# Attention penalties in squares: two penalty products move from GpSimd to ScalarE

## The chip, the cores and the metric

The kernel runs on one core of one Trainium2 chip. The core has a matrix engine (PE), a vector engine (DVE), a scalar engine (ACT), GpSimd (POOL) and a queue that only issues transfers (SP); each works through its own instructions in order, and semaphores tie them together. The metric is the device time of one execution in microseconds, the median of several runs. Lower is better.

## The reference, cut to what matters

The network has four layers, each an attention-like part and a feed-forward part whose outputs are multiplied and added to the residual. The change touches the attention of the last layer only. In the kernel's shapes it handles 16 batches of 256 positions with 128 features in 16 heads of 8:

```python
g = jax.nn.sigmoid(hidden_states @ Wg + bg)
Z_I = g
Z_J = jnp.swapaxes(g, 1, 2)
res = (1.0 - Z_I) * jnp.maximum(1.0 - Z_I - Z_J, 0.0) + Z_I * jnp.minimum(1.0 - Z_I + Z_J, 1.0)
abs_ij = jnp.abs(idx[:, None] - idx[None, :])
scope = jnp.power(s - 2, 1.0 - g) + 2.0 - abs_ij
scope = jnp.clip(scope, 1e-32, 1.0)
log_pen = jnp.log(jnp.maximum(res * scope, 1e-32))
scores = jnp.einsum('bhqd,bhkd->bhqk', q, k) / np.sqrt(HEAD_DIM)
probs = jax.nn.softmax(scores + log_pen[:, None, :, :], axis=-1)
ctx = jnp.einsum('bhqk,bhkd->bhqd', probs, v)
```

One penalty matrix of 256 by 256 serves all 16 heads of a batch. The kernel never takes its logarithm: it multiplies the exponentials by the penalty.

## The kernel before, in words

`attn8` is the loop of all 8-feature attentions; the first layer uses it without a penalty, the last with one. It runs over heads: step `n` of 288 handles head `n` (16 heads a batch, 256 in all) and, 14 heads later, head `m = n - 14` in the second pass.

In step `n`, `scores` lets PE compute raw scores `pa` of head `n` (L345); DVE takes their negated row maxima `nmax` (L366). Once eight heads have their maxima, `shifted` turns them on PE (L387) and DVE adds them into the queries `qa` (L393). For head `m`, PE computes the shifted, transposed scores `pb` (L355) and ACT their exponentials `e` (L376). There are four `pa` and two `pb` buffers. `weaken` multiplies the exponentials of two heads, 128x1024 elements, by the penalty `pen` (L333): POOL does six of a batch's eight pairs, DVE the pairs that start at heads 2 and 8. `weigh` multiplies by the values on PE (L402), ACT copies the result `oT` (L413), and `turn` transposes and divides it (L428, L435, L436). `project` makes queries and keys for two batches: a matmul (L292), a copy on ACT (L299), a store `qkd` to DRAM (L301) and eight loads of `qT` or `kT` (L306), all transfers on the SP queue. `done` multiplies a finished batch by the gate on DVE (L1765) and adds it to the residual on POOL (L1766).

The penalty of batch `b + 1` is made while batch `b` runs. `penalty(b)` returns a list of steps, and the head loop takes one of them after a head's own work, in heads whose number `k` within the batch is in a fixed tuple:

```python
if k in (2, 3, 4, 5, 6, 7, 8, 9, 10, 11, 13, 14) and b + 1 < B:
    parts[b + 1].pop(0)()
elif k == 15 and b + 1 < B:
    pens[b + 1] = parts.pop(b + 1).pop(0)()
```

With `gi` the row of gates (a transfer replicates it over the partitions) and `gj` the negated gate of the partition's own position, the steps are: ACT forms `u = 1 - gi` (`rest`, L1693), `lo = relu(u + gj)` (`low`, L1696, two halves of 256), `hi = relu(gi + gj)` (`high`, L1699, two halves) and `hi = 1 - hi` (`rather`, L1702); POOL forms the distance term `sc` (`near`, L1705), `lo * u` and `hi * gi` (`inner`, L1708) and their sum (`summed`, L1711); DVE takes `pen = min(sc, 1) * lo` (`bounded`, L1715); ACT bounds it from below (`over`, `least_of`, L1719, L1722). A helper, `mixed`, rewrites an access so that the two halves of a row are read alternately, element 0, 256, 1, 257 and so on; `bounded` and the gate product of `done` use it.

A planner orders instructions outside the head loop by its own estimates, so the first two penalties, the setup of the stage and the first projection are interleaved with the last feed-forward work. Inside the loop `pin` fixes the order on every engine as the source writes it.

Of the kernel before, what the change touches and what calls it, by code (L numbers as in the profile page):

```python
# [10 lines left out]
F32 = mybir.dt.float32  # L11
I32 = mybir.dt.int32
BF16 = mybir.dt.bfloat16
AF = mybir.ActivationFunctionType
ALU = mybir.AluOpType
# [4 lines left out]
P = 128  # L20
B = 16
S = 256
D = 128
NT = B * S // P
# [60 lines left out]
def mixed(*tiles):  # L85

    axes = {2: "p (a b) -> p b a", 3: "p t (a b) -> p t b a"}
    return [t.rearrange(axes[len(t.shape)], a=2) for t in tiles]


class Net:
# [140 lines left out]
    def attn8(self, w, bias=None, wout=None, penalty=None, done=None):  # L232
# [12 lines left out]
        nc, tc = self.nc, self.tc  # L245
        scale = 1.0 / math.sqrt(8.0)
        LAG = 14
        H = 16 * B
        with ExitStack() as ctx:
            cp = ctx.enter_context(tc.tile_pool(name="at_c", bufs=1))  # L250
            pool = ctx.enter_context(tc.tile_pool(name="at", bufs=2))
# [18 lines left out]
            for j in range(4):  # L270
                q = cp.tile([P, 4, S], F32, name=f"qT{j}")
                nc.gpsimd.memset(q, 0.0)
                qbuf.append(q)
                k = cp.tile([P, 4, S], F32, name=f"kT{j}")
# [199 lines left out]
            for n in range(H + 4 * 8):  # L474
                i, u = divmod(n, 8)
                m = n - LAG
                if n < H or 0 <= m < H:
                    scores(n if n < H else None, m if 0 <= m < H else None)
                b, half = divmod(i, 2)
                if u == 1:  # L480
                    if is_step(i - 1):
                        shifted(i - 1)
                    if half == 1 and b + 1 < B:
                        values(b + 1)
                elif u == 3:
                    if is_step(i - 4) and penalty is not None:
                        turn(i - 4)
                    if is_step(i - 4) and (i - 4) % 2 == 1:
                        finish((i - 4) // 2)
                    if i % 4 == 2 and i // 4 + 1 < B // 2:  # L490
                        project(i // 4 + 1, 1)
                elif u == 5:
                    if is_step(i - 3):
                        weigh(i - 3)
                elif u == 7:
                    if is_step(i - 3) and penalty is None:
                        turn(i - 3)
                    if i % 4 == 1 and i // 4 + 1 < B // 2:
                        project(i // 4 + 1, 0)
                if done is not None and u in (4, 6) and is_step(i - 4) and (i - 4) % 2 == 1:  # L500
                    done((i - 4) // 2, u == 6)
                if penalty is not None:
                    k = n % 16
                    if k == 0 and b + 2 < B:
                        parts[b + 2] = penalty(b + 2)
                        parts[b + 2].pop(0)()
                    if k in (2, 3, 4, 5, 6, 7, 8, 9, 10, 11, 13, 14) and b + 1 < B:
                        parts[b + 1].pop(0)()
                    elif k == 15 and b + 1 < B:
                        pens[b + 1] = parts.pop(b + 1).pop(0)()  # L510
# [1146 lines left out]
    def attn3(self, g, dr, done):  # L1657


        nc, tc, a = self.nc, self.tc, self.a  # L1660
        with ExitStack() as ctx:
            cp = ctx.enter_context(tc.tile_pool(name="a3_c", bufs=1))
            pool = ctx.enter_context(tc.tile_pool(name="a3", bufs=1))
            pool2 = ctx.enter_context(tc.tile_pool(name="a3_2", bufs=2))
            pool3 = ctx.enter_context(tc.tile_pool(name="a3_3", bufs=3))
            dist = self.const("dist", cp, view="p (k q) -> p k q", k=2)
            least = cp.tile([P, 2], F32, name="least")
            nc.gpsimd.memset(least[:, 0:1], -1e-32)
            nc.gpsimd.memset(least[:, 1:2], 1e-32)
            wide = lambda t: t.rearrange("p (o q) -> p o q", o=1).to_broadcast([P, 2, S])  # L1670

            def penalty(b):

                rows = pool3.tile([P, 2, S], F32, name="rows")
                gi, pw = rows[:, 0, :], rows[:, 1, :]
                u = pool.tile([P, S], F32, name="u")
                lo = pool2.tile([P, 2, S], F32, name="lo")
                hi = pool2.tile([P, 2, S], F32, name="hi")
                sc = pool.tile([P, 2, S], F32, name="sc")
                pen = pool3.tile([P, 2, S], F32, name="pen")  # L1680
                gj = [g[:, 2 * b + k : 2 * b + k + 1] for k in range(2)]

                def fetch():
                    for j in range(2):
                        t = j * NT + 2 * b
                        nc.sync.dma_start(
                            rows[:, j, :],
                            dr[t : t + 2, :].rearrange("t p -> (t p)").partition_broadcast(P),
                        )


                def rest():
                    nc.scalar.activation(u, gi, AF.Identity, scale=-1.0, bias=1.0)  # L1693

                def low(k):
                    return lambda: nc.scalar.activation(lo[:, k, :], u, AF.Relu, bias=gj[k])  # L1696

                def high(k):
                    return lambda: nc.scalar.activation(hi[:, k, :], gi, AF.Relu, bias=gj[k])  # L1699

                def rather():
                    nc.scalar.activation(hi, hi, AF.Identity, scale=-1.0, bias=1.0)  # L1702

                def near():
                    nc.gpsimd.tensor_sub(sc, wide(pw), dist)  # L1705

                def inner(t, by):
                    return lambda: nc.gpsimd.tensor_mul(t, t, wide(by))  # L1708

                def summed():  # L1710
                    nc.gpsimd.tensor_add(lo, lo, hi)  # L1711

                def bounded():
                    to, near, inner = mixed(*(t.rearrange("p k q -> p (k q)") for t in (pen, sc, lo)))
                    nc.vector.scalar_tensor_tensor(to, near, 1.0, inner, ALU.min, ALU.mult)  # L1715


                def over():
                    nc.scalar.activation(pen, pen, AF.Relu, bias=least[:, 0:1])  # L1719

                def least_of():
                    nc.scalar.activation(pen, pen, AF.Identity, bias=least[:, 1:2])  # L1722
                    return pen

                return [
                    fetch, rest, low(0), low(1), high(0), high(1), rather, near,
                    inner(lo, u), inner(hi, gi), summed, bounded, over, least_of,
                ]

            self.attn8(  # L1730
                {n: a["L3_attn_W" + n] for n in "qkv"},
                bias={n: a["L3_attn_b" + n] for n in "qkv"},
                penalty=penalty,
                done=done,
            )


    def layer3(self, end, out):

        nc, tc = self.nc, self.tc
        X = self.xn
        right = lambda n, **kw: tc.tile_pool(name=n, bufs=1, side="right", **kw)
        with ExitStack() as ctx:
            gp = ctx.enter_context(right("a3_g"))
            dram = ctx.enter_context(tc.tile_pool(name="a3_d", bufs=1, space=DRAM))
            with right("f3_w") as cp:
                layers, load = self.local_weights(cp)
                with tc.tile_pool(name="l2_g", bufs=4) as got:  # L1750
                    gather = end["Ga"]
                    end["Ga"] = end["Gb"] = lambda: gather(got)
                    end["wb"] = end["wa"]
                    g, dr = self.local_layers(X, layers, load, end, lambda: self.gates3(gp, dram))
            for c in range(NT // 4):
                xc = X[:, 4 * c : 4 * c + 4, :]
                nc.scalar.activation(xc, xc, AF.Silu)

            def done(b, store):
                ts = slice(2 * b, 2 * b + 2)  # L1760
                if store:
                    nc.sync.dma_start(out[:, ts, :], self.x[:, ts, :])
                else:
                    attn, ffn = mixed(self.s[:, ts, :], X[:, ts, :])
                    nc.vector.tensor_mul(attn, attn, ffn)  # L1765
                    nc.gpsimd.tensor_add(self.x[:, ts, :], self.x[:, ts, :], self.s[:, ts, :])  # L1766

            self.attn3(g, dr, done)
# [516 lines left out]
```

## Time and profile before

| | us |
|---|---|
| median of 3 runs | 2729.04 |
| lowest and highest | 2728.78, 2735.28 |
| the profiled execution | 2734.26 |
| its span, first to last instruction | 2732.50 |
| PE busy | 2346.4 (86%) |
| DVE busy | 1962.1 (72%) |
| ACT busy | 1668.4 (61%) |
| POOL busy | 1384.6 (51%) |

The profile covers one execution. The durations below come from it, while times of kernels are compared by their medians; the profiled execution lies 5.2 us above the median. Busy shares are averages over layers with different limits, so the last attention is read by itself. A row of a group or a tile gives the engine, the line, the operation, the output and the inputs, and how long one instruction took. A row of waits names who waited, for whom, the total, how often, and the longest. In a timeline the two first numbers are start and duration, and brackets give the idle time before the instruction and who ended it. In a row of stretches the columns are the length, the busy time of PE, PE's weight loads, DVE, ACT and POOL with their counts, then the granted clock of PE as a share of full speed, the share of DMA and its rate.

### The profile page before, as it was taken

Reading aid. Unit: us, or ns where it says so; the run is one execution under the profiler, and the core shown is the slowest. Engines: PE = TensorE matmul, PEld = TensorE weight load, DVE = VectorE, ACT = ScalarE, POOL = GpSimd, SP = SyncE. Lnnn points to the kernel's source line nnn. Section 1 sums busy time; section 2 is a strip of 40 time slices with the busy share of each in tenths; the row PEclk is TensorE's granted clock in tenths of the full one; section 3 lists DMA queues with packets and bytes.
Section 4 is the critical chain, followed back from the end, with each engine's and each line's share of the span. In section 5 each row is a group of like instructions: output and inputs, shape, how many; then the busy total and the mean of one; then the engine's idle time right before and its main releaser. Section 6 shows DMA issues by size and latency. Waiting matters only on the chain.

```text
span 2732.5 us, 47736 instructions
## 1 busy us (share of the span) xinstructions
PE 2346.4 (86%) x17672; PEld 1560.2 (57%) x17735; DVE 1962.1 (72%) x3810; ACT 1668.4 (61%) x3680; POOL 1384.6 (51%) x1162
## 2 busy tenths in 40 slices
PE   6999997899756799999983789999999997889887
PEld 4666667566432455555561456666666665655554
DVE  6666633555579688888877899877776662788775
ACT  2555554233235466676641788888999896565653
POOL 3000001422417666666566667565654554798886
PEclk7999998899668899999996999999999998899987
DMA  3001002000114456556552000000000001121210
GB/s 84 24 29 33 17 17 101 6 11 12 35 54 152 142 165 196 180 182 189 173 185 57 21 22 23 15 19 18 24 11 11 13 14 32 33 46 30 49 30 9
DMA packets 136917, 168.25 MB, mean 62 GB/s; under 512 B 20850, under 2 KB 100604, under 8 KB 136684
## 3 DMA queue, kind: packets, MB, share of 16 engines
q1 hardware_dynamic: 128108, 147.09, 18.2%
q0 software_dynamic: 6496, 17.05, 1.8%
q8 instruction: 140, 2.29, 0.4%
q10 hardware_dynamic: 2080, 1.05, 0.1%
q14 instruction: 93, 0.76, 0.1%
HBM read 126.96 MB, written 29.79 MB: 57 GB/s over the span
## 4 chain that ended last, share of the span: by engine, by line
PE 27%; DVE 14%; ACT 11%; POOL 9%; issue 3%; DMA 2%; SPq 1%; POOLq 0%; DVEq 0%; ACTq 0%
PE py L1253 4%; ACT p L2033 3%; POOL e L333 3%; PE pm L2168 2%; PE pm L1922 2%; PE ps L2009 2%; PE ph L1496 2%; DVE pen L1715 2%; PE pa L1098 2%; PE pm L2096 1%; PE py L1519 1%; PE pb L355 1%; PE pa L345 1%; DVE sn L1948 1%; DVE ss L1944 1%
## 5 line engine op out<-in xcount | busy, mean ns | idle before, releaser
L366 DVE TENSOR_REDUCE nmax<-pa 128x2 f32<-128x512 f32 x512 | 329.6, 683 | 135.6 <-PE pb L355 109.1
L376 ACT ACTIVATE e<-pb 128x512 f32<-128x512 f32 x512 | 286.2, 594 | 226.8 <-PE pb L355 204.8
L355 PE MATMUL pb<-qa,kT 32*128 32x256 f32 x2048 | 388.4, 424 | 32.9 <-ACT e L376 32.9
L345 PE MATMUL pa<-kT,qT 32*128 32x256 f32 x2048 | 365.9, 435 | 10.9 <-DMA kT<-qkd 8.2
L1243 POOL TENSOR_TENSOR hc<-st,cn 128x1024 f32<-128x1024 f32 x111 | 261.2, 2353 | 193.7 <-DVE dbb L1226 120.9
L1230 DVE TENSOR_TENSOR_SCAN st<-dab,dbb 128x1024 f32<-128x1024 f32 x128 | 292.7, 2287 | 23.5 <-ACT dab L1216 8.1
L355 PEld LDWEIGHTS pb<-qa,kT 32*128 32x128 f32 x2048 | 249.8, 196 | 62.7 <-ACT e L376 54.0
L345 PEld LDWEIGHTS pa<-kT,qT 32*128 32x128 f32 x2048 | 231.4, 201 | 93.1 <-issue 56.2
L1253 PE MATMUL py<-hc,ident 128*128 128x512 f32 x512 | 270.6, 619 | 8.8 <-DVE hc L1243 7.4
L333 POOL TENSOR_TENSOR e<-e,pen 128x1024 f32<-128x1024 f32 x96 | 229.1, 2394 | 62.7 <-ACT e L376 61.5
L1922 PE MATMUL pm<-qkv,hT 128*128 128x512 f32 x384 | 211.9, 636 | 32.0 <-ACT p L2033 12.2
L2033 ACT ACTIVATE p<-ps,nm,rl 128x128 f32<-128x128 f32 x512 | 230.0, 474 | 12.2 <-DVE nm L2024 11.7
L1216 ACT ACTIVATE dab<-dl,A_log 128x512 f32<-128x512 f32 x256 | 177.7, 718 | 97.2 <-DVE st L1230 56.2
L178 POOL TENSOR_SCALAR ln_r<-ln_mv 128x4 f32<-128x4 f32 x32 | 8.5, 264 | 446.3 <-DVE ln_mv L189 438.6
L1957 POOL TENSOR_TENSOR rot<-rot,sn 128x512 f32<-128x512 f32 x128 | 162.6, 1274 | 125.7 <-DVE sn L1948 125.5
L1226 DVE TENSOR_TENSOR dbb<-du,bn 128x1024 f32<-128x1024 f32 x128 | 187.5, 1465 | 5.5 <-DMA bn<-dr 2.8
L2052 POOL TENSOR_TENSOR p<-p,den 128x512 f32<-128x512 f32 x128 | 130.5, 1041 | 39.7 <-DVE den L2047 30.7
L1253 PEld LDWEIGHTS py<-hc,ident 128*128 128x128 f32 x512 | 92.8, 197 | 80.7 <-issue 61.4
L1519 PEld LDWEIGHTS py<-w,h 128*128 128x128 f32 x752 | 101.1, 197 | 59.2 <-issue 39.7
L402 PE MATMUL pm<-e,vaug 128*32 128x256 f32 x2048 | 129.1, 394 | 3.6 <-DVE s L436 3.6
L1937 ACT ACTIVATE sq<-pm 128x512 f32<-128x512 f32 x128 | 76.4, 597 | 78.5 <-PE pm L1922 71.6
L1510 ACT ACTIVATE h<-ph,b1s 128x256 f32<-128x256 f32 x188 | 78.6, 470 | 70.0 <-PE ph L1496 69.1
(390 smaller groups left out, 5614.5 us busy)
## 6 DMA issues: line engine op xcount, KB each, us to landing
bn<-dr SPq DMA_DIRECT2D x64, 512.0 KB
cn<-dr SPq DMA_DIRECT2D x64, 512.0 KB
w<-in_L_ffn_W_dram SPq DMA_DIRECT2D x94, 256.0 KB
qkd<-qk SPq DMA_DIRECT2D x32, 256.0 KB
v<-v SPq DMA_DIRECT2D x64, 128.0 KB
f_y<-y SPq DMA_DIRECT2D x47, 128.0 KB
f_x<-zero POOLq DMA_DIRECT2D x8, 704.0 KB, 6.7
xr<-f_x SPq DMA_DIRECT2D x44, 128.0 KB
```

The costliest lines, as they stand in the source:

```text
L333: eng.tensor_mul(pairs[m], pairs[m], pen.to_broadcast([P, 2, 2, S]))
L345: nc.tensor.matmul(pa[:, t, :], qbuf[b % 4][r : r + 32, g, ts], kbuf[b % 4][r : r + 32, g, :], start=True, stop=True,)
L355: nc.tensor.matmul(pb[:, t, :], kbuf[b % 4][r : r + 32, g, ts], qas[m // 8][r : r + 32, g % 2, :], start=True, stop=True,)
L366: nc.vector.tensor_reduce(nbuf[n // 8 % 2][:, :, u // 4, u % 4, 8], pa, AX.X, ALU.max, negate=True)
L376: nc.scalar.activation(e, pb, AF.Exp, scale=scale)
L1216: nc.scalar.activation(d["da", r - r % 2][:, r % 2, :], d["dl"][:, h, :], AF.Exp, scale=an[:, h, n : n + 1])
L1226: mul = nc.vector.tensor_mul(db, du, d["bn", n])
L1230: nc.vector.tensor_tensor_scan(wide(d["st", r]), wide(d.pop(("da", r))), wide(db), 0.0, ALU.mult, ALU.add)
L1243: ins = eng.tensor_mul(d["hc", r], d.pop(("st", r)), d["cn", r // 4 * 2])
L1253: nc.tensor.matmul(d["py", h], self.ident, d["hc", r - r % 2][:, r % 2, :], start=(n == 0), stop=(n == N - 1))
L1922: nc.tensor.matmul(pj, hTs[b % 3][:, t * P : (t + 1) * P], rows[b]["l"]["qkv", j], start=True, stop=True,)
L2033: nc.scalar.activation(p[:, c, w, :], rows[b]["ps", u][i][:, c, w, :], AF.Exp, scale=rows[b]["r"][:, w, 0, h + 2 * c : h + 2 * c + 1], bia ...
```

## The change

With `h = gj / 2` and `gj` negative, `(1 - gi) * max(1 - gi + gj, 0)` equals `max((1 + h - gi)^2 - h^2, 0)`, and `gi * max(gi + gj, 0)` equals `max((gi + h)^2 - h^2, 0)`. So both inner terms become a Square with a bias per partition, followed by a Relu with a bias per partition, all on ACT; POOL takes their difference and adds `gi`. The three biases of each position are formed once in a small tile `sides`. The tile `u` and the steps `rest` and `rather` go away, and so do the two products on POOL. `over_none` is one step with two instructions. The list has one step less, so head 11 of a batch no longer takes one.

`bounded` and the gate product of `done` no longer use `mixed`: they read the same elements in plain order.

```diff
-                    if k in (2, 3, 4, 5, 6, 7, 8, 9, 10, 11, 13, 14) and b + 1 < B:
+                    if k in (2, 3, 4, 5, 6, 7, 8, 9, 10, 13, 14) and b + 1 < B:
...
+            sides = cp.tile([P, 3, NT], F32, name="sides")
+            nc.vector.tensor_scalar(sides[:, 0, :], g, 0.5, 1.0, ALU.mult, ALU.add)
+            nc.vector.tensor_scalar_mul(sides[:, 1, :], g, 0.5)
+            nc.vector.scalar_tensor_tensor(sides[:, 2, :], g, -0.25, g, ALU.mult, ALU.mult)
...
-                def rest():
-                    nc.scalar.activation(u, gi, AF.Identity, scale=-1.0, bias=1.0)
                 def low(k):
-                    return lambda: nc.scalar.activation(lo[:, k, :], u, AF.Relu, bias=gj[k])
+                    return lambda: nc.scalar.activation(
+                        lo[:, k, :], gi, AF.Square, scale=-1.0, bias=side(0, k)
+                    )
                 def high(k):
-                    return lambda: nc.scalar.activation(hi[:, k, :], gi, AF.Relu, bias=gj[k])
-                def rather():
-                    nc.scalar.activation(hi, hi, AF.Identity, scale=-1.0, bias=1.0)
+                    return lambda: nc.scalar.activation(hi[:, k, :], gi, AF.Square, bias=side(1, k))
+                def over_none(t):
+                    def f():
+                        for k in range(2):
+                            nc.scalar.activation(t[:, k, :], t[:, k, :], AF.Relu, bias=side(2, k))
+                    return f
...
-                def inner(t, by):
-                    return lambda: nc.gpsimd.tensor_mul(t, t, wide(by))
+                def less():
+                    nc.gpsimd.tensor_sub(lo, lo, hi)
                 def summed():
-                    nc.gpsimd.tensor_add(lo, lo, hi)
+                    nc.gpsimd.tensor_add(lo, lo, wide(gi))
                 def bounded():
-                    to, near, inner = mixed(*(t.rearrange("p k q -> p (k q)") for t in (pen, sc, lo)))
-                    nc.vector.scalar_tensor_tensor(to, near, 1.0, inner, ALU.min, ALU.mult)
+                    nc.vector.scalar_tensor_tensor(pen, sc, 1.0, lo, ALU.min, ALU.mult)
...
-                    fetch, rest, low(0), low(1), high(0), high(1), rather, near,
-                    inner(lo, u), inner(hi, gi), summed, bounded, over, least_of,
+                    fetch, low(0), low(1), over_none(lo), high(0), high(1), over_none(hi), near,
+                    less, summed, bounded, over, least_of,
...
-                    attn, ffn = mixed(self.s[:, ts, :], X[:, ts, :])
-                    nc.vector.tensor_mul(attn, attn, ffn)
+                    nc.vector.tensor_mul(self.s[:, ts, :], self.s[:, ts, :], X[:, ts, :])
```

More of the change, by code (lines that the diff above doesn't have):

```diff
@@ L1675, in penalty @@
                 gi, pw = rows[:, 0, :], rows[:, 1, :]
-                u = pool.tile([P, S], F32, name="u")
                 lo = pool2.tile([P, 2, S], F32, name="lo")
@@ L1680, in penalty @@
                 pen = pool3.tile([P, 2, S], F32, name="pen")
-                gj = [g[:, 2 * b + k : 2 * b + k + 1] for k in range(2)]
+                side = lambda j, k: sides[:, j, 2 * b + k : 2 * b + k + 1]
                 def fetch():
```

## Prediction, made before the changed kernel had run

> **What bounds the kernel now.** The change acts on one stage, the last attention, so I read that stage alone. The page's slices put it in the last 16% of the span; the duration rows of the tile `pen` give its first and last instruction (about 2320 to 2717 us). I then read, in this order: the busy time of the steady part, the waits of each engine there, the timelines of DVE, POOL and ACT around one batch, and the granted clock next to a stall.
>
> ```profile
> 2350.00:2690.00 340.00, 302.30 (x3003) 196.19 (x3002) 273.31 (x392) 195.15 (x370) 298.21 (x154) 0.90 0.15 35
> ACT pen L1719 <- DVE pen L1715: 23.7, 14, 3.0
> PE pb L355 <- ACT e L376: 30.5, 37, 3.1
> POOL e L333 <- ACT e L376: 39.5, 28, 3.5
> DVE pen L1715 <- POOL lo L1711: 7.5, 10, 2.7
> L1715 DVE SCALAR_TENSOR_TENSOR pen<-sc,lo x16: 1087/3225/3241, 2320.3 to 2671.0; 128x512 f32<-128x512 f32 x16
> ```
>
> First row: of 340 us PE is busy 302, DVE 273, ACT 195, POOL 298. No engine is full, so the period (14 batches, spacing of the `qa` instructions on DVE 338.8 us in all, 24.2 us each) is made of waits between in-order queues. The same loop without a penalty, in the first attention, has a spacing of 18.6 to 19.7 us a batch. So the penalty costs about 5 us a batch, and it is not PE's own work. The four waits are links of one chain: POOL's sum releases `pen` on DVE, DVE's `pen` holds ACT's next penalty step, the exponentials stand behind that step on ACT, and PE's `pb` waits for the exponentials.
>
> The last row asks why one instruction takes 1.09 or 3.24 us. The timelines answer:
>
> ```profile
> 2427.78 1.43 POOL L1711 TENSOR_TENSOR lo<-lo,hi 128x512 f32<-128x512 f32 x1
> 2429.16 2.35 POOL L333 TENSOR_TENSOR e<-e,pen 128x1024 f32<-128x1024 f32 x1
> 2431.48 1.47 POOL L1766 TENSOR_TENSOR x<-x,s 128x256 f32<-128x256 f32 x1
> 2429.24 3.23 DVE L1715 SCALAR_TENSOR_TENSOR pen<-sc,lo 128x512 f32<-128x512 f32 x1 [0.54 <-POOL lo L1711]
> 2432.51 0.72 ACT L1719 ACTIVATE pen<-pen,least 128x512 f32<-128x512 f32 x1 [1.77 <-DVE pen L1715]
> ```
>
> POOL finishes the sum and goes straight on to `e`; `pen` starts 0.08 us after it and ends 0.96 us after POOL's `e` has ended. In every overlapped case the duration is the overlap plus 0.96 us. So the two instructions exclude each other, and `pen` loses the race. The same subtraction gives overlap plus 1.09 us for the 1024-element product that DVE does itself (L333). Two kinds of batch occur among the 14: in ten (type A) `pen` first waits for POOL's sum and then for POOL's `e`, as here; in four (type B, 2405, 2452, 2500, 2548) POOL's sum is early, `pen` takes 2.62 us, and POOL's `e` was itself held by ACT's exponential.
>
> ```profile
> 2453.60:2457.00 3.40, 1.85 (x16) 1.02 (x13) 3.40 (x4) 2.13 (x4) 3.40 (x3) 1.00 0.03 10
> 2457.00:2463.90 6.90, 6.90 (x41) 4.69 (x43) 4.59 (x8) 3.15 (x7) 4.33 (x3) 0.51 0.19 54
> 2429.80:2433.20 3.40, 2.35 (x18) 1.00 (x12) 3.40 (x3) 1.29 (x3) 3.40 (x3) 1.00 0.00 0
> ```
>
> Granted clock (third column from the end): after a stretch of 3.4 us in which PE was busy 54%, the next 6.9 us ran at half clock; after one with 69% the clock stayed. There are about 9.5 such half-clock stretches between 2350 and 2690, each just behind a `pen`.
>
> **The change, part by part.**
>
> *POOL.* Per batch `lo*u`, `hi*gi` and the sum (L1708 twice, L1711) become `less` and `summed`: one 512-element instruction fewer, 1.27 us. The new broadcast operand of `summed` is priced as that of L1708 (1.27 us).
>
> *DVE `pen`.* Its operands are read in plain order. The reordered form alone takes 1.09 us; for two SBUF operands of 512 elements in plain order the nearest row is the product at L228, 0.66 to 0.69 us. I take 0.67: 0.42 less. The bounds are 0.55 (half of the 1.09 us net of overlap at L333) and 1.09. The gate product L1765 (0.61 alone at 256 elements) should fall to about 0.37.
>
> *ACT.* Per batch it loses `u` (0.41) and `rather` (0.63) and gains four 256-element Relus at 0.50: 0.97 us more. Squares are priced as the Relus of that shape (L1696, 0.50); the 512-element Square from PSUM (L1937) takes 0.60 against 0.59 for Exp, so I see no surcharge. In the list of steps the heads k get: k=2 +0.09, k=3, 5, 6 nothing, k=4 +0.50, k=7 +0.37.
>
> *A rule against it.* The Trainium skill, ScalarE: Activation LUTs, "Table sets: the hidden batching unit", lists relu, copy, identity and abs as filler in every table set, and does not list Square. If Square shared no set with Exp, its four heads in a batch would each need a load before and after: 8 x 1.28 us (the load's own row) x 14 batches, an estimate of 143 us. The trace speaks against it: the Square of L1937 ran at 2233.42 after a Gelu, with no load before it, and the built program has 119 loads before and after the change. I take zero.
>
> *Setup.* The three 128x32 `sides` instructions (nearest row L1971, 0.18 us) stand in the DVE queue before the stage, where DVE then idles 5.6 us for POOL: zero, or 0.5 us without that cover.
>
> *Start of the stage.* The built order moves the key projection's matmul ahead of some last ffn matmuls, its copy on ACT ahead of a table load and a Silu, and its store `qkd` on the SP queue ahead of the eight loads of `qT`. Now:
>
> ```profile
> 2314.47 2.72 SPq L306 DMA_DIRECT2D qT<-qkd  x8
> 2317.29 0.34 SPq L301 DMA_DIRECT2D qkd<-qk  x1
> 2320.17 2.69 SPq L306 DMA_DIRECT2D kT<-qkd  x8
> 2322.35 8.48 PE L345 MATMUL pa<-kT,qT 32*128 32x256 f32 x40 [8.24 <-DMA kT<-qkd]
> ```
>
> The store waits behind the `qT` loads, then takes 2.9 us to land before `kT` may be read, and PE waits for that. With the store issued at about 2313.7 it lands during the `qT` loads, and `kT` follows them at about 2317.5: 2.6 us earlier, with a query copy some 0.25 us later counted in. Five Relus and Squares that now stand before these copies fill ACT's gaps of 0.7 to 1.2 us there. If they do not fit, the gain falls to about 1 us. The first `pen` is then at about 2319, still ahead of the first `nmax`.
>
> *The sum.* Type A: POOL's chain from `e` (pair 6) to the sum is back to back, and it starts when the exponential of head 7 ends. That exponential is up to 0.45 us later (the k=4 pair of Relus), the chain is 1.27 shorter, so POOL's `e` of pair 12 and with it DVE's lock end 0.8 us earlier; `pen` adds 0.42: 1.22 x 10 = 12.2 us. Type B: 0.42 plus 0.24 from L1765, which holds that `e`: 0.66 x 4 = 2.6. Start: 2.6. Against it the k=7 Relus, where ACT works back to back after a weighing and PE waits for it: 0.37 x 14 = 5.2.
>
> *The clock.* Here row and rule part. The Trainium skill, TensorE: Matmul & The Clock Gate, "Part 1: The HAM clock gate (the "warmup" mystery)", gives an idle window of about 3.4 us as the condition for half clock. No wait in the window above was near that, so by the rule the change would move no half-clock stretch: zero. By the row, 46% idle was enough, and a shorter stall may keep the clock. Batches with a half-clock stretch had a spacing of 24.08 against 23.52 us (four), later 24.6 to 25.7 against 23.15 (about five): about 4 x 0.56 + 5 x 1.5 = 9.7 us for all. I follow the row and take half, 4.9.
>
> Total: -12.2 - 2.6 - 2.6 + 5.2 - 4.9 = -17.1 us. The profiled execution took 2734.26 us (span 2732.50, 1.76 around it), 5.2 above the median of 2729.04; the sum is taken off the median: 2712.
>
> **The rivals.**
>
> *More than that (0.14).* From the end of `pen` to DVE's next arrival there the type A timeline needs 19.8 us. With a stall of 2 us (lock 1.4, own 0.6), no half clock and ACT's pieces in its idle time, the spacing would be 21.9: 14 x 2.3 + 2.6 = 35 us, 2694. ACT's 57% busy share speaks for it; against it, PE's busy share of 89%.
>
> *Relief that is hidden anyway (0.12).* If PE's loop through `pb` and `e` sets the time, POOL's missing instruction only lengthens POOL's wait for `e` (already 39.5 us). What is left is the start and half of the 0.42 us (2.6 + 2.9) against the Relus' 5.2: 2729. The even spacing of half-clock and full-clock batches (0.56 apart) speaks against PE as the bound.
>
> *Slower: ACT becomes the late one (0.14).* At k=4 and k=7 ACT now has 1.0 us of Relu behind each exponential, with two `pb` buffers ahead of it. If every added piece lands on PE's wait for `e`, and POOL's and DVE's savings vanish in that wait and the start does not move, it is 0.97 x 14 = 13.6 us: 2743. It decides from the point where what the exponentials lose exceeds 1.2 us of relief in a batch. For it: PE already waits 30.5 us for `e`. Against it: ACT waits 67.7 us for `pb` in the same part.
>
> **How the numbers follow.** The forecast has 0.60 and spans 2700 to 2726. The range is 2690 to 2736: it takes in most of the first rival, all of the second and the near edge of the third, and leaves out about 0.06 below and 0.12 above. A measurement of this kernel can tell about 0.3% (8 us) from no change. Faster by more: 0.60 x 0.95 + 0.14 = 0.71. Within: 0.03 + 0.12 = 0.15. Slower: 0.14.
>
> **What would show it.** Right: L1715 at 0.67 us alone and at most 2.9 beside POOL; DVE's wait for POOL's sum gone; POOL at about 280 us busy per 14 batches, ACT at about 209; a `qa` spacing near 23.2; fewer half-clock stretches; the first `pa` near 2319.7. Wrong: `pen` still over 3 us (then plain order costs what it was to save); PE's wait for `e` up from 30.5 us, or a table load at a Square (then ACT sets the time); the half-clock stretches more frequent than one a batch; the first `pa` not before 2322.

## The result, and the profile after

The changed kernel has a median of 2696.24 us (2691.41 to 2702.42, six runs) against 2732.82 us for the kernel before (2728.78 to 2740.57, six runs). The ratio is 0.9863, with a 95% interval of 0.9841 to 0.9884: 1.37%, about 37 us faster. The forecast was 2712 us with a range of 2690 to 2736. Direction and range hold; the size of the likeliest case does not. It was 17 us, and the first rival's 35 us came true. 2696 us lies below the 2700 to 2726 us that had been given 0.60; it is inside the range because the range was drawn wide enough to take in most of that rival, not because the sum was right.

The profiled execution took 2702.42 us (span 2700.7), 31.8 us less in span than the one of before. The layers ahead of the stage differ in length from execution to execution, so I don't read the gain from the spans. The clean measure is from the first `qa` of the stage to its last: 2331.91 to 2698.46 before, 2336.14 to 2666.68 after, 366.6 against 330.5 us. So 36.0 us of the gain lie in the loop.

The page after, first the busy times, then the `pb` group (the number behind the second bar is the idle time just before it), and the same group on the page before:

```profile
PE 2335.0 (86%) x17735; PEld 1551.4 (57%) x17735; DVE 1953.6 (72%) x3813; ACT 1677.7 (62%) x3712; POOL 1361.9 (50%) x1146
...
L355 PE MATMUL pb<-qa,kT 32*128 32x256 f32 x2048 | 379.3, 412 | 11.3 <-ACT e L376 11.2
...
L355 PE MATMUL pb<-qa,kT 32*128 32x256 f32 x2048 | 388.4, 424 | 32.9 <-ACT e L376 32.9
```

PE did the same work and was 11 us less busy: its clock was higher. Before, `pb` had sat idle 32.9 us for the exponentials; now 11.2.

The steady part of the stage after, as a stretch, and its waits (who waited, for whom: total, how often, longest):

```profile
2350.00:2660.00 310.00, 292.22 (x3074) 194.37 (x3072) 272.77 (x402) 210.59 (x413) 285.29 (x143) 0.98 0.18 40
```

```profile
POOL e L333 <- ACT e L376: 21.1, 24, 2.9
...
PE pb L355 <- ACT e L376: 9.5, 29, 1.4
...
ACT pen L1729 <- DVE pen L1725: 2.0, 3, 1.3
...
DVE pen L1725 <- POOL lo L1722: 1.4, 1, 1.4
```

The granted clock went from 0.90 to 0.98. All four links of the chain that the prediction started from have shrunk, over 310 us now and 340 then: ACT's wait for `pen` from 23.7 to 2.0, PE's wait for the exponentials from 30.5 to 9.5, POOL's from 39.5 to 21.1, and DVE's wait for POOL's sum from 7.5 to 1.4, with a single case left.

The duration row of `pen` (least, median, longest in ns), and the timelines of POOL, DVE and ACT around one batch of after (start and duration in us):

```profile
L1725 DVE SCALAR_TENSOR_TENSOR pen<-sc,lo x16: 682/2251/2819, 2324.2 to 2642.8; 128x512 f32<-128x512 f32 x16
```

```profile
2448.39 1.28 POOL L1722 TENSOR_TENSOR lo<-lo,rows 128x512 f32<-128x512 f32 x1
2449.61 2.57 POOL L333 TENSOR_TENSOR e<-e,pen 128x1024 f32<-128x1024 f32 x1
...
2450.47 2.26 DVE L1725 SCALAR_TENSOR_TENSOR pen<-sc,lo 128x512 f32<-128x512 f32 x1
...
2452.95 0.71 ACT L1729 ACTIVATE pen<-pen,least 128x512 f32<-128x512 f32 x1
```

POOL's sum ends at 2449.67, and `pen` starts 0.80 us later: DVE, not POOL, arrives last. `pen` still meets POOL's `e` and waits it out: `e` ends at 2452.18, so 1.71 us of overlap and 0.55 us more. Before it was overlap plus 0.96 at an own time of 1.09; now overlap plus 0.55 at an own time of 0.68. The instruction is still three times its own length, but 1 us shorter than the usual 3.23, and ACT waits for it in only 3 cases: here ACT takes up its 0.71 us step 0.22 us after `pen` has ended, without idle time.

### A ledger by batch

Twelve batches, from one `qa` to the `qa` of the same half twelve batches later, first of before, then of after:

```profile
2376.54:2665.92 289.38, 258.22 (x2572) 166.92 (x2569) 235.65 (x337) 170.37 (x324) 256.57 (x134) 0.91 0.16 39
```

```profile
2381.88:2638.41 256.53, 242.52 (x2568) 160.67 (x2568) 227.85 (x338) 177.58 (x348) 238.13 (x122) 0.99 0.19 44
```

Such a row splits a batch's period into three terms. PE's idle time is the length less PE's busy time. The time at half clock is estimated as twice what the clock lacks to 1, times the length; half of it is put down as lost. The rest of the busy time is work at full clock. The clock is taken with the two digits that the row shows, so the clock and work terms are good to about 0.1 us. Before: 24.12 = 19.35 work + 2.17 clock + 2.60 idle. After: 21.38 = 20.00 + 0.21 + 1.17. The loss by the clock is slightly overstated, for the matrix work is the same and its term rose by 0.65: not everything counted as busy stretches with the clock. Putting that 0.65 against the clock, the change brought 1.31 us a batch by clock (1.96 without that) and 1.43 by less idle time.

### The profile page after: what moved, and what is told of

Its sections match the earlier page's. It is cut to its first block, busy times and chain, and to the rows that moved or that the text cites. A ratio compares the mean times of both kernels' runs of the same rounds, so it can differ in the third digit from the quotient of the medians.

```text
span 2700.7 us, 47860 instructions
## 1 busy us (share of the span) xinstructions
PE 2335.0 (86%) x17735; PEld 1551.4 (57%) x17735; DVE 1953.6 (72%) x3813; ACT 1677.7 (62%) x3712; POOL 1361.9 (50%) x1146
## 4 chain that ended last, share of the span: by engine, by line
PE 33%; DVE 14%; ACT 8%; POOL 4%; issue 3%; DMA 3%; SPq 0%; POOLq 0%; DVEq 0%; ACTq 0%
PE py L1253 4%; PE pa L345 3%; PE pb L355 3%; PE pm L2177 3%; PE pm L1931 2%; ACT p L2042 2%; PE pm L402 2%; PE ps L2018 2%; PE ph L1496 2%; PE po L2087 2%; PE pm L2105 2%; PE pa L1098 2%; PE pm L1994 1%; DVE sn L1957 1%; DMA xr<-f_x 1%
## 5 line engine op out<-in xcount | busy, mean ns | idle before, releaser
L355 PE MATMUL pb<-qa,kT 32*128 32x256 f32 x2048 | 379.3, 412 | 11.3 <-ACT e L376 11.2
L345 PE MATMUL pa<-kT,qT 32*128 32x256 f32 x2048 | 357.7, 425 | 9.6 <-DMA kT<-qkd 6.9
L2061 POOL TENSOR_TENSOR p<-p,den 128x512 f32<-128x512 f32 x128 | 130.4, 1039 | 39.5 <-DVE den L2056 30.5
```

The source lines that it names most:

```text
L345: nc.tensor.matmul(pa[:, t, :], qbuf[b % 4][r : r + 32, g, ts], kbuf[b % 4][r : r + 32, g, :], start=True, stop=True,)
L355: nc.tensor.matmul(pb[:, t, :], kbuf[b % 4][r : r + 32, g, ts], qas[m // 8][r : r + 32, g % 2, :], start=True, stop=True,)
```

## The experiments

Two theories run through the expectations, each with what it makes of a run. By the one, the penalty's path through POOL and DVE (called S, P or W in the expectations) is what matters: an instruction less on POOL lets `pen` end earlier, and every engine behind it waits less. By the other, most of the time comes from PE's clock (called C or K): a stall need not be long to cost, because the half-clock stretch behind it costs more. The third rival of the prediction, that ACT's added work takes back part of the gain, is tested on the way.

All together, the ledger by batch taken over the same twelve batches, and the loop from the first `qa` to the last as its difference to before's 366.6 us:

| kernel | median, us | ratio to before (95%) | loop, us | period = work + clock + idle |
|---|---|---|---|---|
| before | 2732.82 | | | 24.12 = 19.35 + 2.17 + 2.60 |
| after | 2696.24 | 0.9863 (0.9841 to 0.9884) | -36.0 | 21.38 = 20.00 + 0.21 + 1.17 |
| e1_plain_only | 2726.76 | 0.9964 (0.9953 to 0.9976) | -10.4 | 23.38 = 19.67 + 1.64 + 2.07 |
| e2_squares_only | 2708.60 | 0.9899 (0.9881 to 0.9918) | -27.8 | 21.98 = 20.00 + 0.44 + 1.54 |
| e3_one_product_less | 2709.05 | 0.9907 (0.9890 to 0.9923) | -26.3 | 22.44 = 19.63 + 0.90 + 1.92 |
| e4_filled_stall | 2727.38 | 0.9972 (0.9959 to 0.9984) | -8.7 | 23.55 = 21.95 + 0.94 + 0.66 |
| e5_pool_again | 2736.25 | 1.0007 (0.9993 to 1.0021) | -1.2 | 23.97 = 19.56 + 1.92 + 2.49 |
| e6_squares_twice | 2727.63 | 0.9975 (0.9955 to 0.9994) | -18.2 | 22.49 = 20.59 + 0.45 + 1.45 |
| e7_late_pen | 2743.53 | 1.0027 (1.0013 to 1.0041) | +9.5 | 24.46 = 19.66 + 2.94 + 1.87 |
| e8_after_filled | 2709.19 | 0.9907 (0.9878 to 0.9935) | -17.5 | 22.89 = 21.98 + 0.23 + 0.68 |
| e9_before_half_filled | 2731.10 | 0.9971 (0.9944 to 0.9997) | -0.4 | 23.51 = 20.79 + 1.18 + 1.54 |
| e10_warm_start | 2697.85 | 0.9856 (0.9833 to 0.9879) | -38.0 | 21.39 = 20.10 + 0.21 + 1.07 |

Each ratio is to the runs of before on the same chip; ledger and loop come from one profiled execution each.

### The two halves of the change, each alone

e1 takes the kernel before and makes only the reads plain:

```diff
-                    to, near, inner = mixed(*(t.rearrange("p k q -> p (k q)") for t in (pen, sc, lo)))
-                    nc.vector.scalar_tensor_tensor(to, near, 1.0, inner, ALU.min, ALU.mult)
+                    nc.vector.scalar_tensor_tensor(pen, sc, 1.0, lo, ALU.min, ALU.mult)
...
-                    attn, ffn = mixed(self.s[:, ts, :], X[:, ts, :])
-                    nc.vector.tensor_mul(attn, attn, ffn)
+                    nc.vector.tensor_mul(self.s[:, ts, :], self.s[:, ts, :], X[:, ts, :])
```

> Kernel before with the two accesses in plain order and nothing else changed: the penalty is still made with two products on POOL. Theory S (the period shrinks by as much as pen ends sooner, the clock worth what I priced, 9.7 us at most): pen about 2.8 us behind POOL's e in type A batches, 2.2 in type B, -0.42 to -0.66 a batch, so 6 to 10 us faster (ratio 0.9965 to 0.998) and nearly as many half-clock stretches. Theory C (most of the gain is the clock that no longer falls): POOL's sum is as late as before, the stall of PE is only 0.4 us shorter, so the half-clock stretches stay and the gain is 5 us or less; if they go, 20 us or more.

e2 is the changed kernel with the lines marked minus above put back: squares alone.

> Changed kernel with the two accesses put back to the alternating order: squares and one POOL instruction less, nothing else. Theory S: POOL's sum comes 0.8 us sooner and ACT has 0.97 us more a batch, so 36 us less the 6 to 10 of plain order, if both add: 26 to 30 us faster (ratio about 0.990). Theory C: the sum no longer releases pen late, stalls of PE fall below what lowers the clock, at most 2 half-clock stretches after 2390 us, 25 to 33 us faster; if the stretches stay, 10 us or less.

They gave 0.36% and 1.01%, which add up to the 1.37% of both. e1's 10 us are at the upper edge of what S allows. e2's 28 us lie in the bands of both theories and do not tell them apart. The waits of e1 between 2350 and 2690 us, then those of e2:

```profile
PE pb L355 <- ACT e L376: 24.5, 38, 2.7
...
ACT pen L1718 <- DVE pen L1714: 16.9, 14, 2.6
...
DVE pen L1714 <- POOL lo L1711: 7.8, 10, 2.7
```

```profile
PE pb L355 <- ACT e L376: 16.8, 42, 1.8
...
ACT pen L1730 <- DVE pen L1726: 7.8, 14, 1.7
...
DVE pen L1726 <- POOL lo L1722: 1.4, 1, 1.4
```

With plain reads alone DVE still waits for POOL's sum (7.8 us, 7.5 before) and the links behind it shrink by 0.4 to 0.5 us a batch, the shorter `pen`. With the squares alone that wait is gone, although `pen` has its old own length.

### What in the squares does it: POOL's instruction, not ACT's

e3 is the kernel before with `hi * gi` left out, so that the second term lacks its factor. POOL has one 512-element instruction less, as in the change; ACT keeps its old work.

```diff
-                    inner(lo, u), inner(hi, gi), summed, bounded, over, least_of,
+                    inner(lo, u), lambda: None, summed, bounded, over, least_of,
```

> Kernel before without the product hi*gi on POOL (that factor is left out of the penalty; its place in the list of steps is kept empty): POOL relieved by the same 1.27 us a batch as in the change, ACT and the access order as before. Theory S: like the squares but without ACT's added 0.97 us a batch, so 5 to 14 us faster than the squares alone, 30 to 40 us in all (ratio 0.985 to 0.989). Rival, that ACT's added work costs nothing: the same time as the squares alone within 0.2%.

It gave 2709.05 us, e2 2708.60: their intervals all but coincide. So the instruction on POOL is worth the whole of e2's gain, and the 0.97 us a batch that the squares add to ACT cost nothing that a measurement can tell. The waits of e3 resemble e2's:

```profile
PE pb L355 <- ACT e L376: 18.5, 39, 1.8
...
ACT pen L1719 <- DVE pen L1715: 10.3, 14, 1.7
...
DVE pen L1715 <- POOL lo L1711: 1.4, 1, 1.4
```

### POOL's instruction given back

e5 is the changed kernel with the distance difference computed twice, 1.27 us a batch more on POOL:

```diff
+                    nc.gpsimd.tensor_sub(sc, wide(pw), dist)
```

> Changed kernel with the distance term computed twice on POOL, so POOL has its 1.27 us a batch back in the same part of the batch, with the squares on ACT and the plain order kept. Theory P (POOL's chain ahead of pen is what the squares relieved): the gain of the squares is lost, about 2727 us, ratio to before 0.995 to 0.998, pen waits for POOL's sum again and takes 2.8 us, the ACT wait for pen is back near 17 us. Rival (POOL now has 21 us of idle time for exponentials in the stage, and only the first steps past the threshold counted): half or less is lost, ratio below 0.992.

It gave 1.0007: the whole 37 us were gone, more than the expectation of P had lost. The `pen` row of e5, its stretch and its waits between 2350 and 2690 us:

```profile
L1726 DVE SCALAR_TENSOR_TENSOR pen<-sc,lo x16: 680/2822/2829, 2325.1 to 2674.9; 128x512 f32<-128x512 f32 x16
```

```profile
2350.00:2690.00 340.00, 305.74 (x3036) 199.24 (x3036) 275.89 (x395) 210.09 (x410) 301.85 (x155) 0.91 0.15 37
```

```profile
PE pb L355 <- ACT e L376: 25.9, 39, 1.8
...
ACT pen L1730 <- DVE pen L1726: 18.6, 14, 1.8
...
DVE pen L1726 <- POOL lo L1723: 8.8, 14, 1.4
```

`pen` waits for POOL's sum in each of the 14 batches again, starts with POOL's `e`, and holds ACT for 1.3 us a batch. The granted clock is back at 0.91. The plain reads remain (own time 0.68) and yet e5 is slower than e1: here ACT's additional work sits behind a late `pen`, and no experiment separates whether that is the reason. What is shown is the size: 1.27 us on POOL cost 2.6 us of period.

### How much room ACT has

e6 is the changed kernel with each Square done twice, 2.0 us a batch more on ACT (`high` is shown, `low` is changed in the same way):

```diff
-                    return lambda: nc.scalar.activation(hi[:, k, :], gi, AF.Square, bias=side(1, k))
+                    def f():
+                        for _ in range(2):
+                            nc.scalar.activation(hi[:, k, :], gi, AF.Square, bias=side(1, k))
+
+                    return f
...
```

> Changed kernel with each of the four Squares of a batch computed twice, 2.0 us of ACT more a batch, at heads 2, 3, 5 and 6. Theory P: ACT is not in the chain, at most 3 us slower than the changed kernel (ratio to before 0.986 to 0.988). The rival from the prediction, that ACT's pieces land on PE's wait for the exponentials: my price of 0.37 for 0.97 us gives 0.8 us a batch or 11 us slower (0.990); all of it on the path would be 28 us (0.9965).

It gave 2727.63 us (2709.24 to 2734.57), 31 us slower than the changed kernel, where hardly anything had been expected. Its waits between 2350 and 2690 us show where it comes in:

```profile
PE pb L355 <- ACT e L376: 18.3, 44, 0.8
...
DVE e L333 <- ACT e L376: 16.5, 14, 1.4
POOL lo L1727 <- ACT hi L1719: 12.8, 13, 1.1
```

DVE's own product now waits 1.2 us for the exponential in every batch (it was 3.8 us in all in the changed kernel), POOL's wait for the squares has doubled (6.1 us in 11 batches in the changed kernel), and PE's wait for the exponentials is 18.3 us where it was 9.5 over 310 us. So the slower rival of the prediction is a real mechanism. The change stays short of it: the first added microsecond on ACT is free, three are not. The spread of e6's runs is wide, and its profiled execution (2718.27 us) is one of the faster ones, so its ledger shows only part of the loss.

### A place where pen was to meet nobody

e7 is the changed kernel with the last three steps of a penalty moved to heads 3, 4 and 5 of the batch that uses it:

```diff
-                    if k in (2, 3, 4, 5, 6, 7, 8, 9, 10, 13, 14) and b + 1 < B:
+                    if k in (3, 4) and b in parts:
+                        parts[b].pop(0)()
+                    elif k == 5 and b in parts:
+                        pens[b] = parts.pop(b).pop(0)()
+                    if k in (2, 3, 4, 5, 6, 7, 8, 9, 10) and b + 1 < B:
                         parts[b + 1].pop(0)()
-                    elif k == 15 and b + 1 < B:
-                        pens[b + 1] = parts.pop(b + 1).pop(0)()
```

> Changed kernel with the last three steps of a penalty (pen on DVE and the two bounds on ACT) moved from heads 13, 14 and 15 to heads 3, 4 and 5 of the next batch, where POOL waits for exponentials; the penalty is needed only at the end of that batch. If the lock with POOL's e still costs what it lasts: pen 0.68 us instead of 2.25, 1.57 x 14 = 22 us faster than the changed kernel (ratio to before about 0.978). If PE, busy 94% now, is the bound: 5 us or less (0.984 to 0.986). Slower if pen collides with POOL's e of head 0 or 4 in the new place.

It was slower than before, 1.0027. The timelines of POOL and DVE around one such place, then the stretch of the loop and one of its waits between 2350 and 2660 us:

```profile
2468.13 2.38 POOL L333 TENSOR_TENSOR e<-e,pen 128x1024 f32<-128x1024 f32 x1 [1.27 <-ACT e L376]
```

```profile
2469.54 1.51 DVE L1727 SCALAR_TENSOR_TENSOR pen<-sc,lo 128x512 f32<-128x512 f32 x1
```

```profile
2350.00:2660.00 310.00, 287.37 (x2690) 191.05 (x2685) 238.47 (x350) 184.71 (x362) 244.73 (x128) 0.87 0.16 38
```

```profile
ACT pen L1731 <- DVE pen L1727: 17.7, 12, 2.0
```

`pen` meets another `e` of POOL (overlap 0.97 us, plus 0.54), the collision that the expectation had named. ACT, which hardly waits for `pen` in the changed kernel, waits for it 1.5 us in each of 12 cases, and the clock falls to 0.87. So this place is worse. A place where `pen` meets no `e` at all was not found, and what it would be worth is open.

### How much of it is PE's clock

e4 is the kernel before with PE kept busy in the stall: the raw scores of two heads of a batch are computed three times instead of once, 1.7 us a batch of unused work.

```diff
+                if penalty is not None and n is not None and m is not None and n % 16 in (0, 1):
+                    b, h = divmod(n, 16)
+                    r, g = 32 * (h % 4), h // 4
+                    for _ in range(2):
+                        for t in range(2):
+                            nc.tensor.matmul(
+                                pa[:, t, :],
+                                qbuf[b % 4][r : r + 32, g, t * P : (t + 1) * P],
+                                kbuf[b % 4][r : r + 32, g, :],
+                                start=True,
+                                stop=True,
+                            )
```

> Kernel before with the raw-score matmuls of heads 0 and 1 of each batch computed three times instead of once, ahead of the pb matmuls that wait (0.85 us of PE work in each, 1.7 us a batch, results unchanged): PE is busy where it stood idle, while the waits of ACT and DVE stay. Theory C: the clock stays full in most batches (granted clock of the stage above 0.95 against 0.90), and the kernel is 15 us faster or more. Theory S: the clock may stay full, but the chain of pen and POOL sets the period: between 5 us faster and 10 us slower.

e8 puts the same lines into the changed kernel.

> Changed kernel with the same extra raw-score matmuls that the filled kernel before had (1.7 us of PE work a batch, results unchanged). It prices the filler where the clock is full anyway. Theory K (the gain is mostly the clock, as PE's account of busy time at full clock, time lost at half clock and idle time says): PE is the bound at 94% busy, so the filler costs nearly all of its 1.7 x 14 = 24 us, less the 1.2 us a batch that PE still idles: 10 to 24 us slower than the changed kernel, ratio to before 0.990 to 0.995, close to the filled kernel before (0.9972). Theory W (POOL's chain and waits alone): PE has slack, at most 5 us slower, 0.986 to 0.988, and the gap of 1.1% between the two filled kernels stays as it is without filler.

There the filler costs 12 us (0.9907 against 0.9863), as K has it. In the kernel before it had gained 8 us, which lies between what C and S had said.

The stretch and three waits of e4, between 2350 and 2690 us:

```profile
2350.00:2690.00 340.00, 329.80 (x3336) 231.34 (x3336) 282.19 (x406) 203.71 (x387) 310.88 (x157) 0.96 0.15 37
```

```profile
ACT pen L1731 <- DVE pen L1727: 25.5, 14, 3.1
...
DVE pen L1727 <- POOL lo L1723: 9.2, 13, 2.7
...
PE pb L367 <- ACT e L388: 5.6, 17, 1.0
```

ACT waits for `pen` no less than before (23.7), and DVE for POOL's sum no less (7.5), yet a kernel with more work is 0.28% faster than before: the clock rose from 0.90 to 0.96. That shows that the half-clock stretches cost time, and that unused matmuls can pay for themselves. It doesn't give their share, for the filler also makes PE the longest queue: idle time is 0.66 us a batch in e4 and 0.68 in e8. Between these two, the ledgers differ in the clock alone (0.94 against 0.23, 10 us over 14 batches), and the loops by 8.8 us. By the medians the gap is 18 us, by intervals of about 3 and 8 us either side. So with PE kept busy the change is still worth 9 to 18 us, against 37 without.

e9 fills half as much in the kernel before (once instead of twice).

> Kernel before with half of the filler: the raw scores of heads 0 and 1 of a batch computed twice, 0.85 us of PE work a batch. Theory K: if that is enough to keep the clock, 12 us of filler are spent instead of 24 and the gain grows from 8 to 12 to 20 us (ratio 0.993 to 0.996); if it is not enough, the half-clock stretches are back and the gain is 5 us or less. Theory W: within 0.2% of the kernel before.

Its interval reaches from 0.9944 to 0.9997, its loop is as long as before's: inconclusive.

### The start of the stage

e10 puts seven unused 512-column matmuls behind the value projection, where PE waits 6.91 us for the first keys, to keep PE busy up to the first `pa`:

```diff
+            if penalty is not None:
+                warm = psm.tile([P, 2 * S], F32, name="pm")
+                for _ in range(7):
+                    nc.tensor.matmul(warm, wqk[0], self.xnT[:, 0 : 2 * S], start=True, stop=True)
```

> Changed kernel with seven extra 128x512 matmuls, whose result is not used, after the first values of the stage, where PE waits 6.9 us for the first keys and its clock then stays at half for 24 us. At full clock the first ten heads take 4.2 instead of 8.4 us on PE, and DVE at 0.68 us a head becomes their limit. If the clock is worth what PE's account says: 4 to 9 us faster than the changed kernel (ratio to before 0.983 to 0.985). If the first heads wait for DVE or the loads anyway: within 3 us of it (0.985 to 0.987).

It gave 2697.85 us, within 2 us of the changed kernel, the second of the two outcomes. PE was busy until just before the first keys (idle 1.70 us instead of 6.91), but the clock fell to half all the same, from 2317.8 to 2331.5 us (in the changed kernel from 2322.7 to 2346.6), behind 3.4 us in which PE was busy 66%. The loop is 2.0 us shorter than the changed kernel's, and the first `pa` comes 17.9 us behind the last normalisation ahead of the stage instead of 16.8. So the filler shortened the half-clock time but did not remove it, and it came with a later start.

## Why the prediction was right or wrong, by its steps

**The mechanism: right, its size: not.** POOL's missing instruction removes the wait for its sum (one case left of ten), plain reads run at 0.68 us (priced 0.67), the two engines still exclude each other, and POOL and ACT are busy 277.8 and 207.2 us in 14 batches (priced 280 and 209). The trace has 119 table loads before and after, and no Square has one.

**Type A and B, priced 14.8 us together: too small.** The step failed where it counted the relief once, as the 0.8 us by which DVE's lock ends earlier. The plain reads had been given 0.42 to 0.66 us a batch, 6 to 9 us, and e1 gave 10. POOL's instruction had been given 0.8 us in ten batches, 8 us, and e3 gave 26 in the loop, 1.7 a batch by the ledger, from an instruction of 1.27 us. The missing part is what the queues behind `pen` pass on: PE's idle time fell by 1.43 us a batch, 20 us over 14 batches where the sum had 14.8 less 5.2, and with it went most half-clock stretches. (In e3 alone idle time fell by 0.68 us a batch and the clock term by 1.27.)

**The clock, priced 4.9 of at most 9.7: the largest miss.** I had compared batches of 24.08 with batches of 23.52 us as if the longer had the half clock. In the changed kernel, with the clock at 0.99, neighbouring batches still alternate, 21.67 and 20.90: every second one has a projection. So the comparison had measured the projection, and the half-clock stretches that it counted first lay in the batches of 23.52 us. By the ledger the clock gave 1.31 to 1.96 us a batch, 18 to 27 us. How much of that the shorter waits would have brought at a steady clock is left open: e4 and e8 bound it only with PE as the bound.

The choice of the row over the rule was right, but the row was read too simply. Two pairs of stretches of the changed kernel:

```profile
2363.70:2367.10 3.40, 1.82 (x13) 1.33 (x14) 3.21 (x4) 2.10 (x5) 3.40 (x2) 0.99 0.02 5
2367.10:2373.90 6.80, 6.80 (x42) 4.54 (x41) 4.26 (x7) 2.82 (x6) 3.88 (x3) 0.50 0.00 0
...
2452.80:2456.20 3.40, 3.09 (x22) 2.14 (x26) 2.69 (x5) 3.04 (x6) 3.40 (x3) 0.94 0.25 66
...
2456.20:2459.60 3.40, 3.40 (x27) 2.40 (x27) 3.40 (x4) 1.61 (x4) 1.79 (x2) 0.56 0.38 55
```

PE busy 54% of 3.4 us, and the next 6.8 us run at half clock. Around another `pen` PE was busy 91%, and the clock fell as well, for about 3.4 us (the 0.94 says that the last part of that stretch already ran at half); in the kernel before it was busy 61% from 2525.3 to 2528.7 us, and the clock stayed. So the busy share alone does not decide it. Neither does the length of `pen`: the first four half-clock stretches of the kernel before that follow 2400 us stand behind `pen`s of type B (2.6 us), none behind those of type A between them (3.2 us), and those of e3 between 2400 and 2640 us stand behind its `pen`s of 1.3 us, none behind those of 2.6. What picks the batch stays open. The Trainium skill, TensorE: Matmul & The Clock Gate, "Part 1: The HAM clock gate (the "warmup" mystery)", asks for an idle window of about 3.4 us. Here PE never idled that long in the loop, and half an idle window was enough, once even a tenth. By the rule the clock would have been worth nothing.

**ACT's Relus, priced +5.2: zero** by e2 against e3. PE's wait for `e`, on which they were to fall, was itself a result of the late `pen`, and shrank with it. The price comes back with 2 us more (e6).

**The start, priced -2.6: -1.5.** From the end of the last normalisation `mh` ahead of the stage to the first `pa` it took 18.3 us before (18.2 and 18.3 in e1 and e3) and 16.8 after (16.7 to 17.0 in e2, e5, e6 and e7). The order of the queue is as foreseen, from the timeline of after:

```profile
2318.20 1.34 SPq L301 DMA_DIRECT2D qkd<-qk  x2
2320.24 2.71 SPq L306 DMA_DIRECT2D qT<-qkd  x8
2323.05 3.42 SPq L306 DMA_DIRECT2D kT<-qkd  x8
2326.70 8.35 PE L345 MATMUL pa<-kT,qT 32*128 32x256 f32 x40 [6.91 <-DMA kT<-qkd]
```

The store no longer stands behind the `qT` loads, but the `kT` loads follow these closely and land slower: from the first issue to the first `pa` 3.65 us, against 2.18 before.

**The rivals.** "More than that" had 2694 us and a spacing of 21.9; measured are 2696 and 21.4. Its three assumptions (short stall, no half clock, ACT's pieces in idle time) all hold, but for two half-clock stretches between 2350 and 2660 us. Against it I had set PE's busy share of 89%. That was the wrong weight: a part of that busy time was the half clock itself. "Hidden anyway" falls with e3, the slower rival with e2.

## What to carry to other kernels

A wait that leaves PE partly idle can be paid twice, as here, once as idle time (2.60 us a batch) and once at half clock (2.17), and the second part shows as busy time: look at the granted clock before you read a high busy share as "near the bound". Split a loop's period into work at full clock, clock loss and idle time, and compare only batches with the same work. Where two engines exclude each other at one place, a short instruction ahead of that place on either of them can be worth more than its length (1.27 us on POOL moved the period by 1.7 us in e3 and 2.6 in e5), and taking it off matters more than what the engine that takes over the work has to do, as long as that engine still has room.

## What the runs showed of the hardware that was not expected

- The loop does not answer in proportion. 1.27 us a batch on POOL cost 2.6 us of period (e5), and 2.0 us on ACT cost 31 us in all (e6), after the first microsecond there had cost nothing.
- The same DVE instruction over the same 512 elements takes 1.09 us when it alternates between the halves of a row and 0.68 us in plain order; the gate product of 256 elements takes 0.61 and 0.42 at its shortest.
- In the changed kernel's loop PE's clock fell to half behind stretches of 3.4 us with PE busy 54% and 91%.
- The parts ahead of the stage, which no kernel here changes by intent, end between 2297.7 us (e10) and 2311.5 us (e2) in the profiled executions. A few microseconds' difference of two spans says nothing of a change in a late stage.
